# A graph network on one core: products into an unread bank in TensorE's planned gaps, and layer 3's statistics eight tiles behind

## The chip, the cores and the metric

The kernel runs on one core of one Trainium2 chip. The metric is the device time of one execution in microseconds, from the first instruction to the last; the number given for a kernel is the median of its executions. Everything is computed in fp32. The engines are called as in the profile: PE is TensorE's matmul, PEld its weight load, DVE is VectorE, ACT is ScalarE, POOL is GpSimd, SP is SyncE. In the profile "PEclk" is the clock that TensorE was granted, 1.0 being full speed.

## What is computed

3125 nodes with 256 features each and 50000 edges, sorted by the node that they lead to, go through four layers. Each layer is a graph part and then a dense part, both added to the node features. The change touches the graph parts of the third layer (called layer 2, counting from 0) and of the fourth (layer 3); between them lies layer 2's dense part, 16 experts of which each node uses two. Cut to these, the reference is:

```python
# layer 2, graph part: attention over the edges into a node
h_s = h @ W_self.T
z = h @ W_func.T
e = leaky_relu(concat([z[edge_src], z[edge_dst], w]) @ W_att.T)
alpha = softmax of e over the edges into one node
agg = segment_sum(alpha[:, None] * z[edge_src], edge_dst)
out = h + relu(where(deg > 0, h_s + agg, h))
# layer 2, dense part: for each node two of 16 experts
y = x + sum over the two of weight * (relu(x @ w1[e] + b1[e]) @ w2[e] + b2[e])
out = layernorm(y) * gamma + beta
# layer 3, graph part: the largest neighbour, then a norm over all nodes
xp = relu(x @ W_proj.T + b_proj)
agg = segment_max(xp[src], dst)          # with a loop edge at each node
out = relu(agg @ W_l.T + b_l + x @ W_r.T)
out = (out - mean(out, axis=0)) * rsqrt(var(out, axis=0) + eps) * gamma + beta
```

Mean and variance of layer 3 run over the nodes, so nothing that uses them can begin before the last node is done.

## The kernel before: tiles, stages and the order of the work

**Tiles.** The nodes lie in 25 tiles of 128, one node to a partition, sorted so that nodes of like degree share a tile. Tile t needs RND[t] rounds: in one round POOL gathers for each of the 128 nodes one neighbour's row out of a table in DRAM, with one indirect DMA (`gather`, L138). RND falls from 32 for tile 0 to 10 and 9 for tiles 23 and 24, and sums to 413; OFF[t] is where tile t's rounds begin in the list of all.

**Layer 2, graph part** (`attend`, L2239). The tiles are taken in the order 24 down to 15, its later chunks, and then 0 upward (`order2`). POOL gathers the rows in blocks of GB = 4, with GR_BUFS = 9 block buffers, so that it can be 36 rows ahead of the last block that DVE has freed. For a tile,

- PE turns the tile (`turned_steps`: two transposes, L1777), ACT copies the result to SBUF (a_xt, L1782), and PE makes the node's own product h @ W_self (L2250, two matmuls of 256 columns, four records in the trace) in the PSUM bank "pu", of which there is one;
- DVE adds up the scores of the edges (L2261 to L2269), ACT takes their exponential (L2271), DVE sums and divides (L2273 to L2276);
- DVE multiplies the node's running sum and adds the own product straight from PSUM (L2278), then adds the gathered rows, one instruction a row (L2283); this frees the blocks of rows. Three more DVE instructions (L2286 to L2288) end the tile.

**Layer 2, dense part.** `route2` (L2291) normalises and routes finished tiles in groups; `experts2` runs the 16 experts in three chunks of tiles (`ex2.run`, matmuls at L1992 and L1996, evacuated by ACT), whose tokens are fetched and put back by indirect DMAs on POOL. The first two chunks run while later tiles are still in `attend`.

**What sets the order.** The instructions of these parts aren't written in the order in which the engines get them. Each part is a generator, a chain; at each step it yields an engine, a cost in microseconds and what it needs. `Plan` (L1702 to L1757) keeps a time `free` for each engine; `run` takes, again and again, the chain whose next step can start first, within 0.05 us the one of lowest rank, emits the instructions of that step and moves the engine's time on by the cost. Some costs are a gather 1.27 us, a matmul 0.0019 us a column (`MM_COL`), the evacuation of a tile by ACT 0.36 to 0.5 us. PSUM banks are `Ring`s: a step that needs a bank can't start before the step that frees the bank's last content. The plan is made when the kernel is built; on the chip each engine goes through its instructions in that order and waits on semaphores. The first call of `pl.run` (L2350) covers `attend`, the routes and most of the experts; a second one (L2361) the rest and `table3`, which writes layer 3's table.

**PSUM** has eight banks in this stage: tp 2, mm 2, y 1, u 2, pu 1. The ring "u" serves the logits (L1835), the routes (L1911, L1984) and `table3`.

**Layer 3, graph part** (L2364 to L2433). 24 gathers are issued ahead (ROWS). Then, tile after tile, PE turns the tile's own features and ACT copies them (`turned`, L1660 and L1662, into g_xt); for each row DVE takes the larger of the sum so far and the gathered row (L2408), and POOL issues the gather 24 rows further on; then the result is turned (g_at), and for each half of the output four matmuls of 128 columns (L2418 and L2420, eight records) and an ACT evacuation with the relu (c_y, L2421) follow. DVE's statistics of a tile, two bn_stats (L2397), read both c_y halves of that tile. They are put among the maxima of a later tile: after row 6 of tile t come those of tile t - LATE, with LATE = 3. The last three tiles' come at the end, ahead of bn_aggr (L2428).

Of the kernel before, what the change touches and what calls it, by code (L numbers as in the profile page):

```python
# [35 lines left out]
ROWS = 24  # L36
W_BUFS = 2
GT = 5
LATE = 3
SLACK = 3.0  # L40
MM_COL = 0.0019
KEEP = max(1, N // 2) - 1
# [55 lines left out]
def tile_gnn_ffn(ctx: ExitStack, tc: tile.TileContext, a: dict, out: bass.AP):  # L98
# [7 lines left out]
    @contextmanager  # L106
    def psums(**bufs):
        with tc.tile_pool(name="psum", bufs=1, space=PSUM) as p:
            before = dict(banks)
            banks["pool"], banks["bufs"] = p, bufs  # L110
            yield
            banks.update(before)

    def ps(tag, shape):
        return banks["pool"].tile(shape, F32, name=tag, tag=tag, bufs=banks["bufs"][tag])
# [504 lines left out]
    def stats(t0, t1):  # L620
        for t in range(t0, t1):
            st = pb.tile([P, 6], F32, name="n_st", bufs=4)[:TN]
            nc.vector.bn_stats(st, xs0[t // 5][:TN, t % 5, :])
            yield
            nc.vector.bn_aggr(mv[:, t, :], st)
            yield
# [1075 lines left out]
    class Plan:  # L1702
# [4 lines left out]

        def __init__(self):
            self.free = {"PE": 0.0, "DVE": 0.0, "ACT": 0.0, "POOL": 0.0, "SP": 0.0, None: 0.0}
            self.wire, self.on, self.chains, self.born = 0.0, None, [], 0  # L1710

        def add(self, rank, chain):
            c = [rank, self.born, chain, None]
# [13 lines left out]
        def run(self, until=None, rings=()):  # L1727

            while self.chains:
                best, end = [], until is not None and until.t is not None  # L1730
                if end and not any(at.t is None for r in rings for at in r.slots):
                    break
                for c in self.chains:
                    engines, us, needs = c[3]
                    if end and any(isinstance(n, Ring) for n in needs):
                        continue
                    needs = [n if isinstance(n, float) else n.t for n in needs]
                    if None in needs:
                        continue
                    for k, engine in enumerate(engines if isinstance(engines, tuple) else (engines,)):  # L1740
                        best.append((max([self.free[engine], *needs]), k, engine, c))
                if not best:
                    raise RuntimeError([str(c[2]) + str(c[3]) for c in self.chains])
                first = min(b[0] for b in best)
                start, _, engine, c = min((b for b in best if b[0] <= first + 0.05), key=lambda b: (b[3][0], b[3][1], b[0], b[1]))
                self.free[engine], self.on = start + c[3][1], engine
                self.resume(c, start + c[3][1] + self.DELAY[engine])

# [409 lines left out]
    tab3 = dram.tile([NP, D], F32, name="tab3")  # L2158

    with tc.tile_pool(name="g2", bufs=2) as gp, \  # L2160
            tc.tile_pool(name="w2", bufs=1) as wp, psums(tp=2, mm=2, y=1, u=2, pu=1):
        ws = load_w(wp, a["L2_gnn_W_self"], "w_s")
        rw2 = load_w(wp, a["L2_ffn_gate_w"], "w_g")
        gb2 = bcast(a["L2_ffn_gate_b"], 16, wp, "w_gb")
# [49 lines left out]
                                                   op0=OP.mult, op1=OP.add)  # L2214
        rounds_beyond(wp, body2)

        order2 = list(range(NT - 1, CH2[2][1] - 1, -1)) + list(range(CH2[2][1]))
        pl = plan[0] = Plan()
        R = {"tp": Ring(2), "mm": Ring(2), "y": Ring(1), "u": Ring(2), "pu": Ring(1)}
        blocks = Ring(GR_BUFS)  # L2220
        xin, rows = {t: At() for t in order2}, {t: [] for t in order2}
        here, done, moved = {t: At() for t in order2}, {t: At() for t in order2}, At()
# [16 lines left out]
        def attend():  # L2239

            for t in order2:
                n = RND[t]
                xn = XN[:, t, :]
                xt = gp.tile([P, 2, P], F32, name="a_xt")
                f = yield from turned_steps(R["tp"], xt, xn, xin[t], 0.36)
                own = yield "PE", 2 * D * MM_COL, (f, R["pu"])
                pfree = R["pu"].take()
                pu = ps("pu", [P, D])
                for k in range(2):
                    nc.tensor.matmul(pu, xt[:, k, :], ws[:, k, :], start=(k == 0), stop=(k == 1))  # L2250
                h = gp.tile([P, D], F32, name="g_u")
                hf = yield "ACT", 0.5, (xin[t],)
                nc.scalar.activation(h, xn, AF.Copy, scale=hasnt[:, t : t + 1])
                e = gp.tile([P, RND[0] + 1], F32, name="g_e")
                nm = gp.tile([P, 1], F32, name="g_nm")
                dn = gp.tile([P, 1], F32, name="g_dn")
                u = ACC[:, t, :]
                while here[t].t is None:
                    yield None, 0.0, (here[t],)
                f = yield "DVE", 0.07, (here[t],)  # L2260
                nc.vector.tensor_copy(e[:, n : n + 1], M[:, t : t + 1])  # L2261
                for r0, m, g, free, landed in rows[t]:
                    f = yield "DVE", 0.14, (landed,)
                    stt(e[:, r0 : r0 + m], g[:, :m, D], q2[:, t : t + 1], ewF[:, OFF[t] + r0 : OFF[t] + r0 + m],
                        op0=OP.add, op1=OP.add)
                f = yield "DVE", 0.51, (f,)
                stt(e[:, :n], e[:, :n], 0.01, e[:, :n], op0=OP.mult, op1=OP.max)
                nc.vector.tensor_reduce(nm, e[:, : n + 1], axis=AX.X, op=OP.max)
                nc.vector.tensor_scalar_mul(nm, nm, -1.0)  # L2269
                f = yield "ACT", 0.3, (f,)  # L2270
                nc.scalar.activation(e[:, : n + 1], e[:, : n + 1], AF.Exp, bias=nm)  # L2271
                f = yield "DVE", 0.71, (f,)
                nc.vector.tensor_reduce(dn, e[:, :n], axis=AX.X, op=OP.add)  # L2273
                stt(dn, den[:, t : t + 1], e[:, n : n + 1], dn, op0=OP.mult, op1=OP.add)
                nc.vector.reciprocal(dn, dn)
                nc.vector.tensor_scalar(e[:, : n + 1], e[:, : n + 1], dn, None, op0=OP.mult)  # L2276
                f = yield "DVE", 0.41, (f, own)
                stt(u, u, e[:, n : n + 1], pu, op0=OP.mult, op1=OP.add)  # L2278
                pfree.t = f
                for r0, m, g, free, landed in rows[t]:  # L2280
                    f = yield "DVE", 0.52 * m, (f,)
                    for r in range(m):
                        stt(u, g[:, r, :D], e[:, r0 + r : r0 + r + 1], u, op0=OP.mult, op1=OP.add)  # L2283
                    free.t = f
                f = yield "DVE", 1.31, (f, hf)
                stt(u, u, has[:, t : t + 1], h, op0=OP.mult, op1=OP.add)  # L2286
                stt(u, u, 0.0, xn, op0=OP.max, op1=OP.add)
                nc.vector.tensor_add(X[:, t, :], X[:, t, :], u)  # L2288
                done[t].t = f
# [51 lines left out]
        with tc.manual_schedule(engines={EN.PE, EN.DVE, EN.Activation, EN.Pool, EN.SP}):  # L2341
            pl.add(2, gathers())
            pl.add(0, attend())
            pl.add(1, route2())
            pl.add(0, ex2.tokens())
            pl.add(0, ex2.weights((blocks, lambda: gp.tile([P, GB, ZW], F32, name="g_rows", bufs=GR_BUFS)
                                   .rearrange("p r d -> p (r d)"), here[order2[-1]])))
            ex2.out = "ACT"
            last = pl.add(4, experts2())
            pl.run(moved, R.values())  # L2350
            ex2.out = "ACT", "DVE"
            ex2.rest(range(NT))
            pl.meet(6.0)
            last[0] = 0
            order3 = ((20, 25), (15, 20), (10, 15), (6, 10), (3, 6), (0, 3))
            pl.add(3, ex2.fetch([t for g in order3 for t in range(*g)]))
            befores = [At(0.0), At(0.0)]
            for i, q in enumerate(order3):
                befores.append(At())
                pl.add(3 + i, table3(range(*q), f"t{i % 2}_", befores[i], befores[i + 2]))  # L2360
            pl.run()  # L2361


    with tc.tile_pool(name="w3", bufs=1) as wp:  # L2364
# [9 lines left out]
        with tc.tile_pool(name="g3", bufs=2) as gp, psums(tp=3, mm=4):  # L2374
# [21 lines left out]
                for i in range(2):  # L2396
                    nc.vector.bn_stats(bs[:, i, t, :], Y[:, i, t * P : t * P + h])  # L2397

            rows = {}
            with tc.manual_schedule(engines={EN.PE, EN.DVE, EN.Activation, EN.Pool, EN.SP}):  # L2400
                for r in range(ROWS):
                    look(r)
                for t in range(NT):
# [3 lines left out]
                    for r in range(OFF[t], OFF[t + 1]):  # L2407
                        nc.vector.tensor_tensor(u, u, rows.pop(r), op=OP.max)  # L2408
                        look(r + ROWS)
                        if t >= LATE and r == OFF[t] + 6:  # L2410
                            stats(t - LATE)
                    at = gp.tile([P, 2, P], F32, name="g_at")
                    turned(at, u)
                    for i in range(2):
# [4 lines left out]
                        for k in range(2):  # L2419
                            nc.tensor.matmul(py, wl[:, k, o], at[:, k, :], start=False, stop=(k == 1))  # L2420
                        nc.scalar.activation(Y[:, i, t * P : (t + 1) * P], py, AF.Relu, bias=bl[:, i : i + 1])  # L2421
                for t in range(NT - LATE, NT):
                    stats(t)


# [129 lines left out]
```

## Time and profile before

| what | value |
|---|---|
| median of 3 runs | 4231.69 us (4225.03 to 4236.29) |
| the profiled execution, its own time | 4194.93 us |
| its span | 4193.1 us |
| mean granted clock of PE over the span | 0.777 |
| layer 2, first gather to the last own product (L2250) | 2057.9 to 2914 us |
| layer 3, first gather to last gather | 3149.6 to 3729.5 us |
| last maximum, last statistics of layer 3 | 3740.0, 3748.1 us |

The profiled execution is 0.9% below the median of the runs. A line of a group reads: source line, engine, operation, output and input by the program's names, shapes, count, then busy microseconds and the mean nanoseconds of one, then how long its engine was idle ahead of these instructions and who ended most of that. A line of the waits reads: who waited, for whom, microseconds in all, times, the longest. In a timeline the bracket gives the idle time ahead of the instruction and what ended it; "remote" and "issue" are waits whose end the profile can't put down to an instruction. A matmul in fp32 leaves two records in the trace. The 40 digits of the clock row are slices of 104.8 us each.

### The profile page before, as it was taken

Reading aid. Unit: us, or ns where it says so; the run is one execution under the profiler, and the core shown is the slowest. Engines: PE = TensorE matmul, PEld = TensorE weight load, DVE = VectorE, ACT = ScalarE, POOL = GpSimd, SP = SyncE. Lnnn points to the kernel's source line nnn. Section 1 sums busy time; section 2 is a strip of 40 time slices with the busy share of each in tenths; the row PEclk is TensorE's granted clock in tenths of the full one; section 3 lists DMA queues with packets and bytes.
Section 4 is the critical chain, followed back from the end, with each engine's and each line's share of the span. In section 5 each row is a group of like instructions: output and inputs, shape, how many; then the busy total and the mean of one; then the engine's idle time right before and its main releaser. Section 6 shows DMA issues by size and latency. Waiting matters only on the chain.

```text
span 4193.1 us, 46658 instructions
## 1 busy us (share of the span) xinstructions
PE 2681.7 (64%) x12940; PEld 2120.1 (51%) x12940; DVE 1935.3 (46%) x7465; ACT 854.3 (20%) x1839; POOL 1758.2 (42%) x1996
## 2 busy tenths in 40 slices
PE   1698999999889999948411366366670111137875
PEld 1576787777777878737310254254540011135653
DVE  4446666665665555442344433334563233245300
ACT  1121223221222233211100022022320000013321
POOL 4333334342253333002466545544337756633323
PEclk9678999989899999978755577577775555557987
DMA  6766455452243444113233355355523323323543
GB/s 220 230 185 205 129 149 159 124 149 63 81 125 102 118 131 128 52 48 107 74 95 93 84 177 177 90 173 173 177 83 104 103 76 91 94 74 109 161 159 101
DMA packets 275970, 521.46 MB, mean 124 GB/s; under 512 B 53608, under 2 KB 176896, under 8 KB 275684
## 3 DMA queue, kind: packets, MB, share of 16 engines
q0 software_dynamic: 105344, 306.57, 25.2%
q1 hardware_dynamic: 159466, 201.07, 15.5%
q10 hardware_dynamic: 10874, 10.54, 0.8%
q8 instruction: 114, 1.87, 0.2%
q14 instruction: 172, 1.41, 0.1%
HBM read 431.19 MB, written 86.78 MB: 124 GB/s over the span
## 4 chain that ended last, share of the span: by engine, by line
another core or an unknown queue 14%; PE 14%; issue 9%; DVE 6%; POOL 3%; DMA 3%; ACT 2%; DVEq 0%; POOLq 0%; ACTq 0%
PE y L1996 5%; PE mm L1992 5%; DVE ACC L2283 2%; DMA xg<-XX,ro_pos 1%; POOL xg L142 1%; PE tp L2047 1%; POOL g_row L138 1%; POOL ro_g L138 1%; PE u L1839 1%; DMA tab<-ACC,idI 1%; PE u L1984 1%; PE mm L2418 0%; ACT ro_h L2073 0%; PE tp L1777 0%
## 5 line engine op out<-in xcount | busy, mean ns | idle before, releaser
L138 POOL DMA_INDIRECT g<-tab,m_si x521 | 498.9, 958 | 978.7 <-DVE mt L897 527.7
L138 POOL DMA_INDIRECT g_rows<-tab,srcI x413 | 402.2, 974 | 287.5 <-DVE ACC L2283 124.6
L138 POOL DMA_INDIRECT g_row<-tab,srcI x413 | 397.7, 963 | 189.3 <-issue 111.1
L887 PEld LDWEIGHTS c<-s,g 128*128 128x128 f32 x2084 | 347.9, 218 | 150.1 <-issue 59.6
L887 PE MATMUL c<-s,g 128*128 128x96 f32 x2084 | 358.2, 301 | 84.1 <-issue 25.5
L894 PE MATMUL pw<-w_d,f 65*128 65x256 f32 x1042 | 375.6, 446 | 13.8 <-DVE mt L897 12.1
L926 PE MATMUL f<-w_rel,aT 128*126 128x256 f32 x1600 | 372.6, 383 | 0.0
L891 ACT COPY aT<-c 128x384 f32<-128x384 f32 (+1 forms) x323 | 236.7, 737 | 596.3 <-PE c L887 395.2
L926 PEld LDWEIGHTS f<-w_rel,aT 128*126 128x126 f32 x1600 | 300.0, 189 | 49.9 <-issue 5.4
L1992 PE MATMUL mm<-ro_xt,ro_w 128*128 128x192 f32 (+3 forms) x928 | 248.7, 420 | 101.9 <-ACT ro_h L2073 61.6
L897 DVE TENSOR_TENSOR mt<-pw,g 128x256 f32<-128x256 f32 x521 | 218.1, 419 | 164.6 <-PE pw L894 85.4
L1996 PE MATMUL y<-ro_w,ro_h 128*96 128x256 f32 (+2 forms) x1040 | 264.9, 410 | 39.9 <-issue 31.5
L2418 PE MATMUL mm<-g_xt,c_wr 128*128 128x128 f32 x200 | 48.6, 387 | 370.0 <-issue 259.3
L1992 PEld LDWEIGHTS mm<-ro_xt,ro_w 128*128 128x128 f32 x928 | 181.4, 218 | 152.1 <-ACT ro_h L2073 66.9
L2408 DVE TENSOR_TENSOR ACC<-ACC,g_row 128x256 f32<-128x256 f32 x413 | 174.0, 424 | 175.4 <-DMA g_row<-tab,srcI 145.2
L1996 PEld LDWEIGHTS y<-ro_w,ro_h 128*96 128x96 f32 (+2 forms) x1040 | 191.5, 190 | 93.2 <-issue 38.3
L2418 PEld LDWEIGHTS mm<-g_xt,c_wr 128*128 128x128 f32 x200 | 40.3, 281 | 377.8 <-issue 262.4
L1044 PE MATMUL w<-w,b_h 128*126 128x256 f32 x800 | 220.6, 401 | 7.3 <-issue 3.7
L142 POOL DMA_INDIRECT xg<-XX,ro_pos x100 | 101.8, 1018 | 292.4 <-issue 135.0
L2283 DVE SCALAR_TENSOR_TENSOR ACC<-g_rows,g_e,ACC 128x256 f32<-128x256 f32 x413 | 200.9, 486 | 47.8 <-DVE ACC L2283 21.6
L1035 PE MATMUL w<-xt,w 128*128 128x252 f32 (+1 forms) x832 | 218.7, 388 | 6.2 <-ACT xt L957 3.2
L894 PEld LDWEIGHTS pw<-w_d,f 65*128 65x128 f32 x1042 | 180.8, 217 | 17.0 <-DVE mt L897 14.2
(578 smaller groups left out, 4558.4 us busy)
## 6 DMA issues: line engine op xcount, KB each, us to landing
ro_w<-in_L_ffn_blocks SPq DMA_DIRECT2D x58, 514.0 KB
ro_w<-in_L_ffn_blocks SPq DMA_DIRECT2D x58, 512.0 KB
f<-in_attr_t SPq DMA_DIRECT2D x521, 32.5 KB
xg<-zero SPq DMA_DIRECT2D x78, 200.0 KB
b_at<-in_edge_attr SPq DMA_DIRECT2D x100, 125.0 KB
tabr<-v SPq DMA_DIRECT2D x12, 758.0 KB
g<-tab,m_si POOLq DMA_INDIRECT x521
g_rows<-in_L_ffn_blocks SPq DMA_DIRECT2D x14, 514.0 KB
```

Of the source, the lines that this page charges most:

```text
L138: return nc.gpsimd.indirect_dma_start(out=dst, out_offset=None, in_=table, in_offset=bass.IndirectOffsetOnAxis(ap=idx, axis=0))
L887: nc.tensor.matmul(pc[:, h, o : o + GW], g[:, h * P : (h + 1) * P], sums[k][0], start=True, stop=True)
L891: nc.scalar.copy(aT[:, :, :, b : b + n * GN].rearrange("p k r n -> p k n r"), pc[:, :, : n * GW].rearrange("p k (n r) -> p k n r", r=16))
L894: nc.tensor.matmul(pw, feats.pop(k), wd, start=True, stop=True)
L897: nc.vector.tensor_tensor(mt[0], pw, rows.pop(k)[:, D:], op=OP.mult)
L926: nc.tensor.matmul(cur["f"][:TN], aT[:, h, r, :], wrel[:, h, r, :], start=(r == 0 and h == 0), stop=(r == 15 and h == 1))
L1035: nc.tensor.matmul(ph, w["01"][:, e, k, i * P : (i + 1) * P], xt[:, k, : n * TN], start=(k == 0), stop=(k == 1))
L1044: nc.tensor.matmul(py, last[:, k, i * TN : (i + 1) * TN], w["02"][:, e - 1, k, :], start=(k == 0), stop=(k == 1))
L1992: nc.tensor.matmul(ph, w[:, o : o + P], xt[:, k, :], start=(k == 0), stop=(k == 1))
L1996: nc.tensor.matmul(py, h[:, i, s], w[:, i * D : (i + 1) * D], start=(i == 0), stop=(i == self.fc - 1))
L2283: stt(u, g[:, r, :D], e[:, r0 + r : r0 + r + 1], u, op0=OP.mult, op1=OP.add)
L2408: nc.vector.tensor_tensor(u, u, rows.pop(r), op=OP.max)
```

## The change

It has three parts.

**Products in gaps.** A function `rest` issues one matmul of the identity with 512 columns of the weights `ws` into a PSUM bank "idle" that nobody reads. While the first plan of layer 2 runs, each time a step for PE is emitted the plan looks at the gap between PE's free time and the step's start, and emits ahead of the step as many of these products as int(gap * 0.6 / 0.9) gives; the plan's time for PE isn't moved by them.

**The bank for it.** "idle" takes the place of "pu". The node's own product now goes into the ring "u", and ACT copies it from there to a tile a_pu in SBUF, with one buffer; DVE's L2278 reads that. The plan's wait for "pu" is gone, and a wait for "u" and a step of 0.42 us on ACT are new.

**The statistics of layer 3.** LATE goes from 3 to 8. A counter `taken` says which tile is next; the three tiles 20 to 22 also take one at row 10 (the condition holds for tiles 20 to 24, but 23 and 24 don't have an eleventh row). So 17 and 3 tiles are taken on the way, and five are left for the end.

```diff
-LATE = 3
+LATE = 8
+FILL = 0.6
...
                 first = min(b[0] for b in best)
                 start, _, engine, c = min((b for b in best if b[0] <= first + 0.05), key=lambda b: (b[3][0], b[3][1], b[0], b[1]))
+                if engine == "PE" and self.rest is not None:
+                    for _ in range(int((start - self.free["PE"]) * FILL / 0.9)):
+                        self.rest()
                 self.free[engine], self.on = start + c[3][1], engine
...
-            tc.tile_pool(name="w2", bufs=1) as wp, psums(tp=2, mm=2, y=1, u=2, pu=1):
+            tc.tile_pool(name="w2", bufs=1) as wp, psums(tp=2, mm=2, y=1, u=2, idle=1):
...
+        def rest():
+            nc.tensor.matmul(ps("idle", [P, 512]), ident, ws.rearrange("p k n -> p (k n)"), start=True, stop=True)
+
...
-                own = yield "PE", 2 * D * MM_COL, (f, R["pu"])
-                pfree = R["pu"].take()
-                pu = ps("pu", [P, D])
+                f = yield "PE", 2 * D * MM_COL, (f, R["u"])
+                free = R["u"].take()
+                pw = ps("u", [P, 2, D])[:, 0, :]
                 for k in range(2):
-                    nc.tensor.matmul(pu, xt[:, k, :], ws[:, k, :], start=(k == 0), stop=(k == 1))
+                    nc.tensor.matmul(pw, xt[:, k, :], ws[:, k, :], start=(k == 0), stop=(k == 1))
+                own = free.t = yield "ACT", 0.42, (f,)
+                pu = gp.tile([P, D], F32, name="a_pu", bufs=1)
+                nc.scalar.copy(pu, pw)
...
                 stt(u, u, e[:, n : n + 1], pu, op0=OP.mult, op1=OP.add)
-                pfree.t = f
...
-            ex2.out = "ACT"
+            ex2.out, pl.rest = "ACT", rest
...
-            ex2.out = "ACT", "DVE"
+            ex2.out, pl.rest = ("ACT", "DVE"), None
...
                         if t >= LATE and r == OFF[t] + 6:
-                            stats(t - LATE)
+                            stats(taken)
+                            taken += 1
+
+                        if t > NT - 6 and r == OFF[t] + 10:
+                            stats(taken)
+                            taken += 1
...
-                for t in range(NT - LATE, NT):
+                for t in range(taken, NT):
                     stats(t)
```

More of the change, by code (lines that the diff above doesn't have):

```diff
@@ L1709, in __init__ @@
             self.free = {"PE": 0.0, "DVE": 0.0, "ACT": 0.0, "POOL": 0.0, "SP": 0.0, None: 0.0}
-            self.wire, self.on, self.chains, self.born = 0.0, None, [], 0
+            self.wire, self.on, self.chains, self.born, self.rest = 0.0, None, [], 0, None
         def add(self, rank, chain):
@@ L2215, in tile_gnn_ffn @@
         rounds_beyond(wp, body2)
+        def rest():
+            nc.tensor.matmul(ps("idle", [P, 512]), ident, ws.rearrange("p k n -> p (k n)"), start=True, stop=True)
         order2 = list(range(NT - 1, CH2[2][1] - 1, -1)) + list(range(CH2[2][1]))
         pl = plan[0] = Plan()
-        R = {"tp": Ring(2), "mm": Ring(2), "y": Ring(1), "u": Ring(2), "pu": Ring(1)}
+        R = {"tp": Ring(2), "mm": Ring(2), "y": Ring(1), "u": Ring(2)}
         blocks = Ring(GR_BUFS)
@@ L2397, in stats @@
                     nc.vector.bn_stats(bs[:, i, t, :], Y[:, i, t * P : t * P + h])
-            rows = {}
+            rows, taken = {}, 0
             with tc.manual_schedule(engines={EN.PE, EN.DVE, EN.Activation, EN.Pool, EN.SP}):
```

## The prediction

> **What bounds the kernel now.** I read the page first (engines, clock row, groups), then the waits of layer 2's stage (2060 to 2910 us) and of layer 3's (3150 to 3760), then a table by stretches, and last the timeline around one wait that the others could not explain.
>
> ```profile
> span 4193.1 us, 46658 instructions
> ...
> PE 2681.7 (64%) x12940; PEld 2120.1 (51%) x12940; DVE 1935.3 (46%) x7465; ACT 854.3 (20%) x1839; POOL 1758.2 (42%) x1996
> ...
> PEclk9678999989899999978755577577775555557987
> ...
> L138 POOL DMA_INDIRECT g_rows<-tab,srcI x413 | 402.2, 974 | 287.5 <-DVE ACC L2283 124.6
> L138 POOL DMA_INDIRECT g_row<-tab,srcI x413 | 397.7, 963 | 189.3 <-issue 111.1
> ```
>
> No engine is busy all the time; the work moves from one limit to the next. The clock row shows two stretches at half clock: slices 21 to 23 (2096 to 2411 us) and 31 to 36 (3145 to 3774). They lie in the two stages in which POOL fetches neighbours' rows, 413 in each: the two group lines. A gather takes 0.96 to 0.97 us and follows the last at 1.25 to 1.27 us when nothing stops it (the 0.3 us of "issue" lie between), so 413 of them are a floor of about 520 us for each stage. Layer 3's run from 3149.6 to 3729.5: 580 us, so some 60 us are stops.
>
> ```profile
> core 0: us, PE busy (x) PEld busy (x) DVE busy (x) ACT busy (x) POOL busy (x), PEclk, DMA share, GB/s
> 2060.00:2200.00 140.00, 25.08 (x74) 17.38 (x74) 60.38 (x186) 10.81 (x30) 96.00 (x99) 0.50 0.37 101
> 2200.00:2300.00 100.00, 18.46 (x42) 9.56 (x41) 51.38 (x171) 5.38 (x18) 67.99 (x78) 0.50 0.34 92
> ...
> 3150.00:3400.00 250.00, 25.39 (x102) 21.51 (x102) 71.24 (x172) 6.29 (x17) 174.79 (x183) 0.52 0.33 96
> ```
>
> In both, PE is busy 10 to 18% of the time at a clock of 0.50 to 0.52. POOL, with its 0.3 us between gathers, is the engine that is nearly full. What stops it is in the waits, layer 2's first and then layer 3's:
>
> ```profile
> DVE g_dn L2273 <- ACT g_e L2271: 148.0, 14, 39.3
> POOL g_rows L138 <- DVE ACC L2283: 124.6, 19, 34.4
> ...
> PE pu L2250 <- DVE ACC L2278: 62.5, 2, 33.6
> ```
>
> ```profile
> ACT c_y L2421 <- remote: 300.0, 21, 22.0
> ...
> DVE c_bs L2397 <- ACT c_y L2421: 125.3, 14, 26.9
> DVE c_bs L2397 <- issue: 119.9, 8, 22.4
> ...
> POOL g_row L138 <- DVE ACC L2408: 75.8, 60, 20.0
> ```
>
> POOL stands behind DVE, because DVE frees the row buffers; in layer 3 DVE stands behind ACT in the statistics (L2397), and ACT behind something "remote". The timeline of ACT there, and POOL's first gather after a stop:
>
> ```profile
> 3362.23 0.37 ACT L2421 ACTIVATE c_y<-mm,c_bl 128x128 f32<-128x128 f32 x1 [21.96 <-remote]
> 3381.14 0.37 ACT L2421 ACTIVATE c_y<-mm,c_bl 128x128 f32<-128x128 f32 x1 [18.54 <-remote]
> ...
> 3411.93 0.37 ACT L2421 ACTIVATE c_y<-mm,c_bl 128x128 f32<-128x128 f32 x1 [17.07 <-remote]
> 3412.70 0.37 ACT L2421 ACTIVATE c_y<-mm,c_bl 128x128 f32<-128x128 f32 x1 [0.40 <-remote]
> ```
>
> ```profile
> 3382.43 1.01 POOL L138 DMA_INDIRECT g_row<-tab,srcI  x1 [20.03 <-DVE ACC L2408]
> ```
>
> By the records PE had done this work by 3344.1, yet its semaphores came 18 to 22 us apart. One such interval stands for 8 records, so about 2.8 us a record, against modelled durations of 0.3 to 0.4. A few us after POOL stops, the lateness is gone (3412.70 follows at once). I find the same at POOL's other stops in layers 2 and 3. Late signals begin 7 to 12 us into a back-to-back stream of gathers, where PE is asked for more than some 0.36 records a us (layer 3: 0.39); in layer 2's first 270 us, with 0.28 to 0.32, there are none. Whether the stream causes them isn't shown.
>
> [...]
>
> **Part 1, the fill.** It is cast when the plan sees PE idle: int(gap x 0.6/0.9) products, so a gap of 1.5 us is the least. From 2060 to 2330 PE is busy about 55 us and idle 215; 215 x 0.667 = 143, less rounding about 130. Later, to 2970, gaps are shorter: 50 to 60. One product is 128x512, two records of 512 columns. The nearest row has half the columns: L926's 1600 records of 128x256, two to a product and overlapping, keep PE busy for 372.6 us at a clock of 0.9 and more, 0.466 us a product. Twice that is an estimate of 0.9 us warm, and 1.8 at half clock. So it fills 0.6 of a gap warm and 1.2 of one cold. By busy time alone it would be nearly hidden: 130 x 0.9 = 117 us in 215. What isn't hidden: TensorE takes its instructions in order, so a product that is late holds up the next tp and pu; and the fill brings records from 0.3 to over 1 a us, well over the 0.36 beyond which signals come late under a stream. At layer 3's rate, 0.36 a us, the 260 records of the fill alone would need 720 us. That can't pile up: 36 rows are gathered ahead (GR_BUFS 9 by GB 4), 46 us at 1.27. Then DVE waits for the product at L2278, frees nothing, POOL stops, and the signals come in 7 to 20 us later. Cycles of 46 + 10 to 12 us in 270 us are 4.7 stops of 10: **+45 us** in the first stretch. From 2330 to 2970 POOL has about ten such stops already, and each gets one or two products of 1.8 us longer before the queue is through: **+25 us**. Bounds for the fill: above, stops as long as the longest seen (34.4) in place of 10, 4.7 x 34.4 = 160 less what overlaps, about +150; below, if a warm clock takes the late signals away, most of the 124.6 us of POOL waiting for L2283 can be won, about -100. The value taken is +70.
>
> **Part 2, the product of the tile's own row through ACT.** Removed: the bank "pu" and its wait, 62.5 us in 2 waits of PE; at clock 0.50 PE had no other ready work then, so nothing comes of it, and who is late next is still DVE's chain. Added: 25 copies 128x256 at 0.37 us (the row of a_xt's copies, median 372 ns): 9.3 us on an engine 20% busy, hidden in its waits; not hidden they are 9. The copy needs the one a_pu buffer free, that is L2278 of the tile before: ACT waits perhaps 1 to 2 us there, with the experts' evacuations behind it and their matmuls behind these. [...] The ring "u" is now shared with logits and routes: one more user of two banks, 25 times under 1 us. **0**, bounds -5 and +12.
>
> **Part 3, the statistics later.** They wait for c_y (125.3 + 119.9 us on DVE), and POOL's long stops, 20.0, 7.5, 13.4, 9.2 and 8.8 us, each end just after such a wait: 59 us. Eight tiles are some 130 rows, 165 us, against a lag of PE of up to 112 us: most waits go. But signals at 2.8 us a record make 20 records a tile 56 us, while a tile's rows take POOL 16.5 x 1.254 = 21 us. If POOL doesn't stop, PE falls behind by 35 us a tile, and the cover of eight tiles lasts 8 x 21 / 35, about five tiles instead of two; so DVE stops again perhaps twice, 14 to 20 us. Gained: 39 to 45. Given back at the end: 17 + 3 tiles are taken (the extra one fires at tiles 20 to 22 alone, since tiles 23 and 24 have 10 and 9 rows), 5 are left instead of 3, and PE's backlog is then 7 or 8 tiles. At the end tiles follow each other by 2.8 us (statistics at 3741.1, 3743.9, 3746.7), so the tail grows from 8 us to 20 to 24: +14. No DMA and no gather moves against another on POOL's queue. **-28**, bounds -55 (all stops gone, no longer tail) and 0.
>
> **Sum.** +45 + 25 + 0 - 28 = **+42 us**, 1.0%. Against the profiled execution, 4194.9 us (span 4193.1 and 1.8 around it), that is 4237; the median of the runs shown, 4231.7, lies 0.9% above the profiled one, and the forecast is put on it: **4274 us**.
>
> **Rivals.** (a) *The fill does what a warm clock should*: records of L2250 at 0.38 us, their shortest, instead of the median 0.63, and signals in time; -45 of fill on top of -28: 4159. For it: clock 0.50 throughout, and 171.9 us of PE's weight loads for L2250 begin after an unexplained "issue". Against: from 2500 to 2600 us the clock is 0.82 and the signals under POOL's streams are late all the same. (b) *The fill hides wholly*, layer 3 gains: 4204. For it: 215 us of idle PE for 117 us of warm products. This decides if late signals need something other than PE's rate. (c) *The two cancel, or layer 3 gives nothing* because PE's late signals are its true bound (56 against 21 us a tile) and the tail takes the rest: 4232. (d) *PE becomes layer 2's bound*, with stops of 30 us rather than 10: +150 - 28, about 4354; it decides once a product costs over (215 + 45) / 130 = 2.0 us, when the fill no longer fits into the gaps and the stops together.
>
> **Chances.** Forecast 0.40, (d) 0.12, (a) 0.22, (b) 0.16, (c) 0.10. So slower 0.52, same 0.10, faster 0.38, with 0.3% (12.7 us) as what a measurement of this kernel can tell from no change. The range leaves out the better half of (a), about a tenth, and the far part of (d), under a tenth: 4172 to 4370. If it is slower, 4245 to 4370.
>
> **What would show it.** Fill: the clock over 0.7 from 2060 to 2330 whichever way it goes; right if PE's signals come late there, with "remote" before ACT's a_pu copy and POOL's wait for L2283 above 124.6 us; the stage ends after 2950 rather than at about 2914. Wrong if POOL's gathers of tiles 24 to 15 keep their pitch of 1.27. Part 2: 25 copies of 0.37 us and L2278 not waiting for ACT. Part 3: DVE's waits before L2397 under 60 us before the last row, POOL's stops under 25, layer 3's gathers within 545 us, the tail over 16. The prediction is wrong in sign if the fill costs under 28 us, and wrong in kind if late signals vanish under a warm clock.

## The result, and the profile after

The changed kernel takes 4258.4 us (median of 4 runs, 4255.0 to 4265.0) against 4228.4 us before on the same chip (4 runs, 4223.9 to 4236.3): a ratio of 1.0074, 95% interval 1.0054 to 1.0095, some 30 us slower. The forecast was 42 us slower.

One thing has to be known for all that follows, and it was not known when the forecast was made. The kernel before takes about 4190 to 4230 us on some chips and 3745 us on others; whether that is the chip or the hour can't be told, since each chip was seen in one condition. I call the first kind **late** and the second **prompt**, for a reason shown below. The first traces, of before and after, are from late chips. A ratio always compares runs on one chip.

The page of after:

```profile
span 4263.3 us, 47402 instructions
...
PE 2873.2 (67%) x13308; PEld 2154.6 (51%) x13308; DVE 1932.1 (45%) x7465; ACT 860.4 (20%) x1864; POOL 1768.7 (41%) x1996
...
PEclk9778999999899999959676778778875555567987
...
L139 POOL DMA_INDIRECT g_rows<-tab,srcI x413 | 400.1, 969 | 323.0 <-DVE ACC L2292 144.0
L139 POOL DMA_INDIRECT g_row<-tab,srcI x413 | 413.5, 1001 | 176.0 <-issue 95.8
...
L2222 PE MATMUL idle<-w_s,ident 128*128 128x512 f32 x368 | 249.1, 764 | 136.0 <-remote 70.0
```

368 records are 184 products. The clock row no longer shows half clock in slices 21 to 23: it rose. Yet POOL's idle time ahead of layer 2's gathers grew from 287.5 to 323.0 us. By stretches:

```profile
core 0: us, PE busy (x) PEld busy (x) DVE busy (x) ACT busy (x) POOL busy (x), PEclk, DMA share, GB/s
2060.00:2200.00 140.00, 71.49 (x120) 23.10 (x120) 48.97 (x147) 8.14 (x22) 89.75 (x96) 0.66 0.35 95
2200.00:2300.00 100.00, 72.78 (x170) 27.38 (x169) 51.48 (x181) 11.74 (x34) 50.99 (x61) 0.81 0.24 67
```

The clock went from 0.50 to 0.66 and 0.81, PE's busy time from 44 to 144 us in these 240 us, and POOL did 157 instructions instead of 177. Who waits, from 2060 to 2910 us:

```profile
DVE g_dn L2283 <- ACT g_e L2281: 165.9, 12, 37.4
ACT a_pu L2260 <- PE u L2257: 138.2, 12, 53.0
POOL g_rows L139 <- DVE ACC L2292: 130.5, 11, 24.4
...
PE idle L2222 <- remote: 70.0, 14, 21.3
```

In the kernel before, L2278 is the instruction that needs the own product; by its trace PE cost it 0.5 us of waiting in all, and DVE's long waits stood at the exponential already (148.0 us). Now ACT waits for the own product at its copy (L2260), and the exponential stands behind that copy in ACT's queue, so what the own product costs turns up in DVE's wait at L2283 (165.9 us). PE in a stretch with products, and POOL's gather that came after it:

```profile
2143.23 2.07 PE L2222 MATMUL idle<-w_s,ident 128*128 128x512 f32 x2 [21.26 <-remote]
2148.83 2.07 PE L2222 MATMUL idle<-w_s,ident 128*128 128x512 f32 x2 [3.53 <-remote]
2155.12 2.08 PE L2222 MATMUL idle<-w_s,ident 128*128 128x512 f32 x2 [4.22 <-remote]
2160.03 2.07 PE L2222 MATMUL idle<-w_s,ident 128*128 128x512 f32 x2 [2.83 <-remote]
2162.84 6.86 PE L2222 MATMUL idle<-w_s,ident 128*128 128x512 f32 x8 [0.74 <-PE idle L2222]
```

```profile
2175.41 1.07 POOL L139 DMA_INDIRECT g_rows<-tab,srcI  x1 [21.07 <-DVE ACC L2292]
```

While POOL gathers (it stopped at 2154.3), products follow each other by 5.6 and 6.3 us; 8 us after it stopped, four take 6.86 us together, and only then the own product starts (2169.53), although its input a_xt was ready at 2138.67; ACT copies it, and DVE frees the rows. 5.6 us for two records is the 2.8 us a record of layer 3's c_y in the first trace. And layer 3 after, 3205 to 3830 us:

```profile
ACT c_y L2435 <- remote: 347.1, 20, 22.1
...
DVE c_bs L2406 <- ACT c_y L2435: 84.4, 18, 21.1
POOL g_row L139 <- DVE ACC L2417: 70.5, 98, 26.3
...
DVE c_bs L2406 <- issue: 51.9, 5, 21.4
```

DVE's waits ahead of the statistics went from 245.2 to 136.3 us, but not under the 60 that I had named. Where POOL stood, in the traces from late chips (a stop is a pause of POOL over 3 us while layer 2's gathers run, over 1 us in layer 3's):

| trace | layer 2's gathers, first to last | stops | layer 3's gathers | stops | last gather to the next stage's first fetch |
|---|---|---|---|---|---|
| before | 851.6 us | 244.5 | 580.8 | 58.9 | 52.0 |
| after | 903.4 | 299.6 | 582.0 | 43.0 | 61.8 |

Layer 2 has 15 stops in both, nearly all at the same gathers. The first four (up to 2334 us before, 2379 after) went from 42.3 to 84.8 us, the other eleven from 202.2 to 214.8. The two traced executions are 70 us apart, the timed medians 30, so these differences overstate the cost. (One correction to the text above the prediction: `attend` takes the tiles 24 down to 6 and then 0 to 5.)

### The profile page after: what moved, and what is told of

Read it like the earlier page. It is cut to its first block, busy times and chain, and to the rows that moved or that the text cites. A ratio compares the mean times of both kernels' runs of the same rounds, so it can differ in the third digit from the quotient of the medians.

```text
span 4263.3 us, 47402 instructions
## 1 busy us (share of the span) xinstructions
PE 2873.2 (67%) x13308; PEld 2154.6 (51%) x13308; DVE 1932.1 (45%) x7465; ACT 860.4 (20%) x1864; POOL 1768.7 (41%) x1996
## 5 line engine op out<-in xcount | busy, mean ns | idle before, releaser
L139 POOL DMA_INDIRECT g_rows<-tab,srcI x413 | 400.1, 969 | 323.0 <-DVE ACC L2292 144.0
L139 POOL DMA_INDIRECT g_row<-tab,srcI x413 | 413.5, 1001 | 176.0 <-issue 95.8
L2222 PE MATMUL idle<-w_s,ident 128*128 128x512 f32 x368 | 249.1, 764 | 136.0 <-remote 70.0
L2292 DVE SCALAR_TENSOR_TENSOR ACC<-g_rows,g_e,ACC 128x256 f32<-128x256 f32 x413 | 201.0, 487 | 39.3 <-DVE ACC L2292 15.1
```

Source lines behind the costliest of these rows:

```text
L139: return nc.gpsimd.indirect_dma_start(out=dst, out_offset=None, in_=table, in_offset=bass.IndirectOffsetOnAxis(ap=idx, axis=0))
L2222: nc.tensor.matmul(ps("idle", [P, 512]), ident, ws.rearrange("p k n -> p (k n)"), start=True, stop=True)
```

## Experiments

**Before again.** No edit; on a prompt chip, as it turned out.

> The kernel before, once more, for a trace and a spread from the same chip as the next three. All theories: ratio 1.000 within 0.2 per cent. Its layer 2 (first to last gather of a neighbour's row) 830 us, layer 3's gathers 580 us, as in the first trace; if the first trace, 34 us under the median of the runs shown, was an unusual one, the difference must show in one of the stages here.

Measured: 3745.5 us, ratio 1.000 (0.9988 to 1.0012). Layer 2's gathers take 610.4 us instead of 851.6, layer 3's 516.2 instead of 580.8, without one stop. Layer 3's ACT, and POOL's row of the page:

```profile
2877.17 0.37 ACT L1662 COPY g_at<-tp 128x256 f32<-128x256 f32 x1 [49.07 <-PE tp L1660]
2878.88 0.37 ACT L2421 ACTIVATE c_y<-mm,c_bl 128x128 f32<-128x128 f32 x1 [1.34 <-PE mm L2420]
2880.58 0.37 ACT L2421 ACTIVATE c_y<-mm,c_bl 128x128 f32<-128x128 f32 x1 [1.34 <-PE mm L2420]
```

```profile
L138 POOL DMA_INDIRECT g_rows<-tab,srcI x413 | 401.8, 973 | 126.3 <-issue 104.5
```

Here c_y's second half comes 1.70 us after the first, where it was 18 to 22 us, and the second one 4.2 us after its tile's last maximum, where it was up to 112. The granted clock is the same 0.50 in layer 2's first 200 us, gathers take the same 0.97 us, and the rows' packets the same 153 ns on average. So the late signals are no feature of the program. The two traces of the kernel before are 440 us apart: 241 in layer 2's gathers, 65 in layer 3's, the other 134 in other stages.

The prediction speaks of TensorE's signals alone, but on late chips DVE's own results come late as well. This is the first stop in the trace of before, 9.3 us:

```profile
2148.45 0.17 DVE L2268 TENSOR_REDUCE g_nm<-g_e 128x1 f32<-128x13 f32 x1 [1.23 <-DVE g_e L2267]
...
2155.46 0.23 DVE L2276 TENSOR_SCALAR g_e<-g_e,g_dn 128x13 f32<-128x13 f32 x1 [1.24 <-DVE g_dn L2275]
2156.92 0.48 DVE L2278 SCALAR_TENSOR_TENSOR ACC<-ACC,g_e,pu 128x256 f32<-128x256 f32 x1 [1.23 <-DVE g_e L2276]
...
2160.42 1.07 POOL L138 DMA_INDIRECT g_rows<-tab,srcI  x1 [9.33 <-DVE ACC L2283]
```

DVE's small instructions wait for DVE's own last result and start 1.4 to 1.5 us apart; no wait for PE is recorded in that chain. On the prompt chip the only wait of DVE for DVE in layer 2's gathers is one of 0.5 us.

**The fill alone**, LATE at 3 again, on that chip.

```diff
-LATE = 8
+LATE = 3
...
-                        if t > NT - 6 and r == OFF[t] + 10:
+                        if False:
```

> The changed kernel with layer 3's statistics three tiles behind as before (LATE = 3), so the products in the gaps and the new way of the own product alone. Theory (the products make PE's signals late, each stop of POOL in layer 2 longer): slower by 30 to 60 us, layer 2's gathers 50 to 60 us longer. Rival A (the ACT copy and the shared ring cost it): as slow as this, and the next kernel too. Rival B (the loss sits in layer 3, with the later statistics): within 10 us of before.

Measured: 1.0005 (0.9994 to 1.0016), no stops. Layer 2's first 200 us:

```profile
2003.00:2100.00 97.00, 77.26 (x150) 26.22 (x150) 51.08 (x157) 11.17 (x29) 73.77 (x76) 0.88 0.42 111
2100.00:2200.00 100.00, 78.42 (x178) 28.43 (x177) 58.35 (x194) 9.98 (x32) 77.69 (x88) 0.88 0.39 107
```

The theory fails. The number is rival B's (within 10 us), but there is no loss in layer 3 either: the clock is 0.88 in place of 0.50, PE is busy 77 to 78% of the time, and nothing gets faster or slower. POOL's stream is the bound (610.9 us, 610.4 without the fill), and the higher clock was worth nothing next to it.

**The bank and ACT's copy alone**, the same with FILL = 0.0.

> As the last, but with FILL = 0: no products, only the own product through the ring u and ACT's copy. Theory: within 8 us of before. Rival A: slower by 25 us or more.

Measured: 0.9999 (0.9988 to 1.001). Rival A falls on a prompt chip. On a late one this was not run alone, and every run of the fill contains the bank and the copy.

**The later statistics alone**, LATE = 8 with its counter in the kernel before.

> The kernel before with layer 3's statistics eight tiles behind and nothing else. As predicted: 28 us faster (0.7 per cent). Rival, read from the trace of after, where layer 3's gathers take 582 us as against 580 and the tail is 10 us longer: 0 to 12 us slower, POOL's stops fewer but its gathers 1.40 us apart from the ninth tile on.

Measured: 1.0001 (0.9992 to 1.001), still the prompt chip: it has no stops to save, so neither the 28 us nor the rival is tested by this.

**The whole change**, same chip.

> The changed kernel itself, whole, against before. In the four runs just made, before took 3745 us in place of 4228, no signal of TensorE was late and no stream of gathers in layers 2 and 3 stopped. If the change costs what it costs only where TensorE's signals are late, then with before at about 3745 us the ratio is 1.000 within 0.2 per cent, since each part alone gave that; with before at about 4228 us it is 1.007 again. If the parts cost something together that none costs alone, it is over 1.003 in either case.

Measured: 0.9998 (0.9985 to 1.001). On this chip the change costs nothing; its cost shows only on chips where signals are late.

**More products**, to see where they stop being free. On another prompt chip (before 3744.3 us).

```diff
-FILL = 0.6
+FILL = 1.2      # the next: 2.4
```

> As the run with the fill alone (statistics three tiles behind), FILL = 1.2 in place of 0.6, so twice the products, about 370. A product then costs, against the gap it was planned for, what one of 1.8 us would with FILL = 0.6. At a warm clock 1.33 x 0.87 us is 1.16 of a gap, so PE runs late in the planned gaps. Theory (the fill costs time only when PE can't get through it in its gaps, and then by stops of POOL): 10 to 60 us slower, stops of POOL in layer 2, where there are none with 0.6. Rival (the chain through PE has slack enough): within 6 us of before.

> The same with FILL = 2.4, about 740 products: as if one cost 3.5 us, still under the 5.6 us that two records at the 2.8 us of the first traces' layer 3 would take. Theory: PE is the bound of the stretches with gaps; 740 x 0.87 = 640 us of products in some 300 us of gaps, so 250 to 350 us slower, with POOL stopping after each 36 rows ahead. Rival: under 60 us slower.

Measured: 404 products, 1.0288 (1.0259 to 1.0317), 108 us; 858 products, 1.1638 (1.1587 to 1.1688), 611 us. Stops are back. POOL's waits in layer 2 with FILL = 2.4:

```profile
POOL g_rows L139 <- DVE ACC L2292: 365.2, 25, 86.8
POOL xg L143 <- ACT ro_ct L1983: 126.9, 2, 66.4
```

The direction is the theory's, both sizes are well above it. One reason is that a product costs more than 0.87 us: in the next run 45 in a row take 53.1 us, 1.18 each. Another is their number, 404 and 858 for some 370 and 740. At 1.18 us, FILL = 0.6 is 0.79 of a gap and 1.2 is 1.57. Between them lies the point from which the fill costs on a prompt chip; no run finds it.

**Layer 3 with PE kept late by work**, on that chip, statistics three and eight tiles behind.

```diff
+                    for _ in range(45 if t < 12 else 0):
+                        nc.tensor.matmul(ps("idle", [P, 512]), ident, wl.rearrange("p k n -> p (k n)"), start=True, stop=True)
                     at = gp.tile([P, 2, P], F32, name="g_at")
```

> The kernel before, with 45 products of 128x512 that nobody reads in each of layer 3's first 12 tiles, ahead of the tile's second transpose, so that PE takes about 44 us for a tile whose rows take POOL 40 down to 20 us: PE late by work, as it was in the first traces by its signals. Statistics three tiles behind. Worked out: DVE waits in tile 14 for tile 11's c_y at 12 x 44 = 528 us, so POOL stops, and layer 3's gathers end about 660 us after their start in place of 517: 120 to 180 us slower. If POOL's gathers come 1.40 us apart whenever DVE, and not POOL, is behind, they do so here after each stop; if that belonged to the chip of the first traces, they stay at 1.25.

> The same load with the statistics eight tiles behind. Worked out: DVE waits in tile 19 instead, for the same 528 us, and 57 rows are left rather than 130: layer 3's gathers end about 575 us after their start, 50 to 100 us slower than before and 60 to 100 us faster than the last kernel. Rival (the gain is given back at the end, as the trace of after has it: stops shorter by 16 us, gathers slower by 16, tail longer by 10): within 20 us of the last kernel.

Measured: 1.0771 (1.0733 to 1.0809) with three, 1.0515 (1.0481 to 1.0549) with eight; eight is 96 us the faster, as worked out. The load was 55 us a tile and not 44, so both are slower than expected: 287 and 191 us above the kernel before. POOL's waits in layer 3, three and then eight:

```profile
POOL g_row L138 <- DVE ACC L2408: 304.0, 72, 35.4
```

```profile
POOL g_row L138 <- DVE ACC L2408: 208.3, 46, 39.2
```

So where PE is late by plain work, tiles of cover do save POOL's stops. The question of the pace gets a double answer. For the first five or six gathers after a stop, while DVE works off its backlog, most gathers take 1.07 us and come 1.38 apart, here as in the trace of before; then DVE has caught up, and they come 1.25 apart again. And 90 records in 53 us, under a back-to-back stream of gathers, have no late signal on this chip: the prediction's "0.36 records a us" is no threshold of the hardware.

**Other traffic in layer 3**: copies of 12.8 MB, queued on SP ahead of layer 3's loop; the chip was a late one (before 4191.7 us).

```diff
+            for j in range(4):
+                far = dram.tile([400, 8000], F32, name=f"far{j}")
+                nc.sync.dma_start(far, a["edge_attr_64"].rearrange("(p t) d -> p (t d)", p=400))
```

> The kernel before, with four copies of the edge attributes (12.8 MB each) from DRAM to DRAM queued on SP at the start of layer 3's graph part; nothing reads them. It asks whether other traffic makes TensorE's signals late, as they were in the first traces and not in the later ones. If so, c_y follows a tile's last maximum by tens of us, where it takes 4.2 without the copies. If not, that lag stays under 10 us, whatever the copies do to the landing of the gathered rows (layer 3 may be longer by up to 300 us for that). I expect the second, since in the two traces of before the packets of the gathers took 153 ns each, the same in both.

Measured: 4335.2 us, one run. Inconclusive: the copies did not fall into layer 3, where the DMA engines are busy 0.33 of the time as before; layer 2 began 140 us later instead. Its layers 2 and 3, whose instructions are those of before, serve as a second trace on a late chip: 859.7 and 583.6 us of gathers, 254.5 and 64.3 us of stops.

**One and a half times the products**, FILL = 0.9, on the same late chip.

> The fill alone with FILL = 0.9, between 0.6, which cost nothing here, and 1.2, which cost 108 us. In the last runs one product of several in a row took 1.18 us (45 of them 53.2 us), so FILL = 0.9 takes 1.18 of a gap, 0.6 takes 0.79 and 1.2 takes 1.57. If the fill costs time as soon as it is longer than the gap, and by what it is longer, a third of the 0.57 at 1.2: about 35 us slower, 20 to 60. If it needs a backlog of 36 rows first: within 6 us of before.

Measured: 290 products, 1.0202 (1.0175 to 1.023), 83 us. Layer 2's gathers take 932.3 us, 73 more than on the same chip without products; stops 327.1 us. It does not answer the question asked of a prompt chip, but it gives the dose on a late one: with the same bank and copy, 290 products cost 83 us, and the 184 of the next run 27.

**The fill alone once more**, on a third late chip (before 4223.3 us).

> The fill alone with FILL = 0.6 and the statistics three tiles behind, once more. On a chip on which before takes about 4200 us and TensorE's signals are late: 15 to 45 us slower, less than the 83 us that FILL = 0.9 cost on such a chip; the stops of POOL in layer 2 some 40 us longer in all; layer 3's gathers 580 us and its tail 8 us, so that the whole change costs about 10 us more than this. On a chip with before at about 3745: 1.000 within 0.2 per cent, as before.

Measured: 1.0061 (1.0041 to 1.008), 27 us. Layer 2's gathers 897.7 us, stops 292.5; layer 3's gathers 585.0, stops 63.8, 47.5 us to the next fetch. Who waits in layer 2:

```profile
POOL g_rows L139 <- DVE ACC L2292: 145.7, 13, 24.9
...
ACT a_pu L2260 <- remote: 103.6, 5, 49.2
...
PE idle L2222 <- remote: 85.6, 21, 20.2
```

The fill, with its bank and copy, has nearly the whole loss of the changed kernel (1.0061 of 1.0074). The rest, some 5 us, is not clear of zero, as the intervals overlap and the chips differ. How the 27 us divide between products and copy isn't separated, but the dose above and the four products ahead of the own product in the trace of after point to the products.

## Why the prediction was right, and where it was not

**The sign and the kind were right, the size in part by luck.** 42 us were forecast and 30 measured. But the fill alone, put at 70, cost 27 in a timed run, and the later statistics, put at a gain of 28, gained nothing; the two errors nearly cancel. The kind is as forecast: the fill makes a late PE later, the own product comes late, DVE frees no rows, POOL's stops get longer (299.6 us in layer 2 where it was 244.5). The number of products (184, forecast 180 to 190), PE ahead of a_pu's copy and the end of the stage after 2950 came as named. That keeping PE busy raises the clock was the author's estimate; from 2060 to 2330 PE was busy 45.1 us at a clock of 0.50 in before and 154.6 us at 0.70 (named as over 0.7) in after. The runs with more products show on a prompt chip that a backlog of PE brings POOL's stops (365.2 us of waits for L2292 with FILL = 2.4).

**"+45 us" for the first stretch** was met by the trace's 42.5, but by another road. The prediction had 4.7 new stops of 10 us, one for each 36 rows, on a stretch without late signals. The trace has the same four stops as before, at the same gathers, each 7 to 14 us longer. Two readings were wrong. PE was busy 45 us of the 270 and not 55. And the prediction's own table has 74 and 42 records in 140 and 100 us, 0.53 and 0.42 a us and not 0.28 to 0.32, and the stretch had late results already: its four stops, 42.3 us in before, are gone on a prompt chip, and by the profile the first hangs on DVE's own results.

**"+25 us" for the later stretch** was double of what the traces show, 12.6. The stops there stand behind several engines, and a longer flush was mostly hidden.

**"+70 us" for the fill together** was mis-sized: 55 us of stops between the two traces, 27 us in the timed run of the fill alone. The trace of before comes from an execution of 4194.9 us, 33 us under the 4228.4 that it is compared with, so part of the 55 may belong to that execution; which stage made up those 33 us is open, as there is no second trace of before from that chip. A product is also dearer than 0.9 us: 1.18 us in a row on a prompt chip, where by the profile the next product's weight load waits for the last product (135 us in 135 waits of PEld in the fill alone, 1.6 at most), and 5 to 6 us when results are late. That the whole costs no more fits the limit that the prediction gave: once POOL stops, PE catches up (8 us after the stop at 2154.3, four products in 6.86 us).

**"0" for the bank and the copy** held on a prompt chip and is open on a late one. What it missed is the exponential behind the copy in ACT's queue: the copies of after waited 138.2 us for PE, 53.0 at the longest. Its lower bound, -5, was the author's estimate, and the traces show no such gain: DVE's instruction that reads the own product takes 484 ns (median) from a_pu in after, 480 from "pu" in PSUM in before.

**"-28 us" for the later statistics failed.** The step was: the stops go, "the cover of eight tiles lasts about five tiles instead of two", two stops of 14 to 20 us remain, the tail grows by 14. POOL ran 321 gathers instead of 169 before its first long stop, and PE fell behind by 30 us a tile (35 forecast), so this part was right. But PE catches up only while POOL stops: in after each c_y came 22.4 to 33.8 us after the last one from 3500 to 3646, 1.5 to 2.6 us after it from 3661 to 3668, as POOL's stop of 26.3 us had ended (at 3659.6), and then 23.3 and 21.7 us after it. The lag of a tile's c_y behind its last maximum grew to 224 us at tile 7, where it had been 112 at most, and the stops came later instead of vanishing: 43.0 us, against 58.9 to 64.3 in four traces with three tiles. And those 16 to 21 us were lost on the way. From row 150 on, DVE and POOL mostly took turns:

```profile
3545.94 0.43 DVE L2417 TENSOR_TENSOR ACC<-ACC,g_row 128x256 f32<-128x256 f32 x1 [0.98 <-DVE ACC L2417]
3546.23 1.10 POOL L139 DMA_INDIRECT g_row<-tab,srcI  x1 [0.30 <-DVE ACC L2417]
3547.34 0.43 DVE L2417 TENSOR_TENSOR ACC<-ACC,g_row 128x256 f32<-128x256 f32 x1 [0.97 <-DVE ACC L2417]
3547.64 1.09 POOL L139 DMA_INDIRECT g_row<-tab,srcI  x1 [0.31 <-DVE ACC L2417]
```

Here each maximum waits about 1 us for DVE's own last one, begins as a gather ends and reaches into the next one, which takes 1.09 us, and gathers come 1.40 us apart instead of 1.25: 150 of them, from row 150 to row 300, took 207.9 us, 20 more than at 1.254. The rows had landed 1 us and more before, so it isn't the data. Gathers beside DVE's work are slower on a prompt chip too (1.07 us, above); what it doesn't have is the wait of DVE for itself (95.3 us in 103 waits in layer 3 of after), which keeps DVE from catching up. Layer 3's gathers therefore took 582.0 us, in the middle of the four traces with three tiles (580.8 to 585.0), and the way from the last gather to the next stage grew to 61.8 us from 45 to 52. This is read from one trace of the later statistics on a late chip; there the part wasn't run alone. That cover as such works is shown by the two loaded runs: where PE is late by plain work, eight tiles were worth 96 us.

**The rivals.** (a), a clock that cures the late signals, fell: the clock rose on late chips (0.70) and they stayed late. On prompt chips it rose (0.88) and was worth nothing (1.0005). (b), a fill that is hidden, is what prompt chips show, without a gain in layer 3. (c) was nearest for layer 3: it gives nothing, and its tail is 10 us longer. (d), PE as the bound, is what FILL = 2.4 makes of a prompt chip, where PE is busy 96% of layer 2's gathers.

**What stays open** is why results of TensorE and DVE are late on some chips. The granted clock, the gathers' pace, the time of a packet and PE's load don't tell the two kinds apart: they are alike in both (0.50 at layer 2's start, 0.97 us a gather, 153 ns a packet) or were varied. That PE and DVE catch up some us after POOL stops (PE after 8 us in the stretch of after shown above) points to the stream of gathers or its transfers, and no run here separates these from other causes.

## What to carry to other kernels

Here, where POOL's stream set the time, products that kept TensorE's clock up were worth nothing: raising the clock from 0.50 to 0.88 moved the time by 0.05%, within the noise. On a prompt chip they were free at 0.79 of the planned gaps (FILL = 0.6) and cost 108 us at 1.57 (FILL = 1.2), and on late chips one took 5 to 6 us in place of the planned 0.9. Before cover is added against a wait, ask what ends the lateness: if it is the very stop that the cover removes, as the one trace of the later statistics on a late chip has it, the cover lets the backlog grow: there c_y's lag rose from 112 us at most to 224.

## What the runs showed of the hardware that was not expected

- One program takes 3745 us on some chips and 4190 to 4230 on others, with the same granted clock of 0.50 in layer 2's start. On the slower ones TensorE's results come at about 2.8 us a record while POOL gathers back to back; on the others c_y follows the last maximum by 4.2 us. DVE's results are late too: in layer 2 of before the instructions that add the rows wait for each other 32 times, 21.6 us in all, and on a prompt chip never.
- 128x512 products in fp32 into one PSUM bank, one after the other at a granted clock of 1.00, take 1.18 us each (in after, 13 records in 7.70 us from 2170.61) and not twice the 0.466 us of L926's 256 columns.
- While DVE adds up rows beside them, gathers take 1.07 to 1.09 us instead of 0.95 on both kinds of chip. On a prompt chip DVE worked off 14 rows in 6.25 us and POOL was back at its pace; on a late chip the two took turns in one trace, one row a gather, 1.40 us apart.
